# The last layer's main operations in one fixed order on three engines, with shorter forms at the ends of its rows

## The chip, the core and the metric

The kernel runs on one core of a Trainium2 chip. The metric is device time in microseconds (us) from the start of the program to its end. The engines are PE (TensorE: matrix products and transposes), DVE (VectorE: elementwise work and reductions), ACT (ScalarE: functions such as Ln and Exp, scaled copies), POOL (GpSimd) and SP (SyncE), which issues DMAs here. Each engine runs its own list of instructions in the order in which the program was emitted, and waits on semaphores for what other engines produce.

## What is computed

Four graph layers follow each other on x of 4096 rows and 64 features, with one 4096 x 4096 matrix adj in all of them. Each ends in `x = layernorm(x + layer(x))`. The change lies in the fourth layer and in the layernorm ahead of it. The fourth is a graph layer on the Poincare ball (c = 1):

```python
def _logmap(x, y, c):
    sub = _mobius_add(-x, y, c)
    sub_norm = jnp.maximum(jnp.linalg.norm(sub, axis=-1, keepdims=True), MIN_NORM)
    ...
    arg = jnp.clip(sqrt_c * sub_norm, 0.0, TANH_CLIP)
    return 2.0 / (sqrt_c * lam_x) * jnp.arctanh(arg) * sub / sub_norm
...
deg = jnp.maximum(adj.sum(axis=1, keepdims=True), 1e-08)
w = adj / deg
log_ij = _logmap(x[:, None, :], x[None, :, :], c)
agg = jnp.einsum('ij,ijc->ic', w, log_ij)
transformed = agg @ weight + bias
return _expmap(jnp.zeros_like(transformed), transformed, c)
```

So every pair (i, j) of the 4096 nodes needs a factor, a function of the distance of the two points; adj is multiplied by the factors, and the products with x are summed over j. The exponential map at the origin is tanh(|v|) v / |v|.

## The kernel before

**Layers 1 to 3** fill the first 957 us and are not touched, but for the layernorm behind layer 3. That is done for two groups of 512 rows at a time by ends() (L1397): summed (L1410) takes mean and variance by bn_stats and bn_aggr, roots (L1432) takes Ln and Exp on ACT, rest (L1436) refines the root by one step on DVE and applies it. Two of its four calls run as steps of a list called seam in the gather stage of layer 3, the other two as steps of the last layer's loop.

**The last layer's tiles.** The 4096 rows form eight groups of 512. The pairs form a triangle of 8 x 8 tiles of 512 x 512: row i of the triangle holds a diagonal tile (i, i) and the tiles (i, j) to its right, so there are rows of 8, 7, ... 1 tiles, 36 in all. The factor is symmetric, so a tile's factors serve twice: as they are, with adj's tile "own" (at_d), and transposed, with adj's opposite tile "mirrored" (at_m).

**Units.** A tile is worked in two units of 256 x 512, held as [128, 2, 512] (1024 elements in each of 128 partitions; the second unit of a diagonal tile has 512). The loop at L1846 takes one unit n an iteration, 72 in all, and works on several at once:

- product(n) (L1615): PE gives v, a bilinear form of the two points, in one of two PSUM places.
- square(n) (L1632): ACT writes w = v squared.
- opposite(n) (L1639): PE adds a term to v for the diagonal sign.
- less_one(n) (L1655): DVE lowers w by one and floors it.
- L1858, L1859: ACT takes Ln of w, then rt = Exp(0.5 Ln w), the root.
- L1883: DVE adds v and rt (in rt), after which v's place is free for product(n + 2).
- L1885: ACT turns w into Exp(-0.5 Ln w). L1894: ACT takes Ln of rt; in the program's text this is done for unit n - 1 at the end of iteration n.
- L1868: DVE forms the factors f = min(rt, T_MAX) w, for unit n - 2. L1871: DVE multiplies at_d by f.
- turn(t, h) (L1664): PE transposes f, eight blocks of 128 x 128 in an iteration (L1680, or L1673 on the diagonal), and DVE multiplies at_m by the result in PSUM (L1682, L1675).
- gather (L1685): PE sums own and mirrored products into one PSUM bank (L1696, L1704, L1708). ACT copies the mirrored half to tb (L1715) once a tile, and the row's own half at the end of the row (L1719).

The PSUM places: two for v (two banks each), three of one bank for transposes and all small products (tag "post"), one for the sums.

**Row ends.** When a row is complete, finals(g) (L1772) puts six steps on seam, and each iteration runs one: first (products with the weight), second (adds the bias), third (squares and norms by Ln and Exp), fourth (tanh as 1 - 2 / (1 + Exp 2|v|)) and fifth, which calls layernorm (L273) with by_ln and by_scale and issues the output's DMA on SP. The last three groups end after the loop (L1907).

**What sets the order.** A scheduler of the framework places the instructions of each engine; it keeps the data dependencies, and may move anything else. in_order() (L213) keeps an instruction in the program's order. behind(engine, ins) (L1387) adds a dependency without a semaphore on the instruction that was last passed to behind for that engine, so that all of them keep the order of the program's text. Before, only the start of the layer goes through behind: product for n < 2, opposite and less_one for n < 1, and the first instructions of ends().

Of the kernel before, what the change touches and what calls it, by code (L numbers as in the profile page):

```python
# [9 lines left out]
F32 = mybir.dt.float32  # L10
# [27 lines left out]

TANH_ONE = 20.0
# [23 lines left out]
def gnn4_kernel(  # L63
# [74 lines left out]
    nc.vector.memset(one_col, 1.0)  # L138

# [133 lines left out]
    def layernorm(dst, y, by_ln=False, by_scale=False):  # L273

        st = sm.tile([P, GB, 6], F32, name="ln_st")
        mv = sm.tile([P, GB, 2], F32, name="ln_mv")
        for b in range(GB):
            nc.vector.bn_stats(st[:, b, :], y[:, b, :])
            nc.vector.bn_aggr(mv[:, b, :], st[:, b, :])
        ve = sm.tile([P, GB], F32, name="ln_ve")  # L280
        s = sm.tile([P, GB], F32, name="ln_s")
        r = sm.tile([P, GB], F32, name="ln_r")
        nc.vector.tensor_scalar_add(ve, mv[:, :, 1], LN_EPS)
        if by_ln:
            nc.scalar.activation(s, ve, AF.Ln)
            nc.scalar.activation(s, s, AF.Exp, scale=0.5)
        else:
            nc.scalar.activation(s, ve, AF.Sqrt)

        nc.vector.reciprocal(r, s)  # L290
        nc.vector.tensor_tensor(r, ve, r, ALU.mult)
        nc.vector.tensor_tensor(s, s, r, ALU.add)
        nc.vector.reciprocal(r, s)
        nc.vector.tensor_scalar_mul(r, r, 2.0)
        if by_scale:
            nc.vector.scalar_tensor_tensor(s, mv[:, :, 0], -1.0, r, ALU.mult, ALU.mult)
            for b in range(GB):
                nc.scalar.activation(dst[:, b, :], y[:, b, :], AF.Identity, bias=s[:, b : b + 1], scale=r[:, b : b + 1])
            return
        nc.vector.tensor_tensor(dst, y, over_rows(mv[:, :, 0]), ALU.subtract)  # L300
        nc.vector.tensor_tensor(dst, dst, over_rows(r), ALU.mult)

# [1094 lines left out]
    def ends(two):  # L1397
# [12 lines left out]
        def summed(ps_p):  # L1410
# [19 lines left out]
            nc.vector.tensor_scalar_add(ve, mv[:, :, 1], LN_EPS)  # L1430

        def roots(ps_p):  # L1432
            nc.scalar.activation(s, ve, AF.Ln)
            nc.scalar.activation(s, s, AF.Exp, scale=0.5)

        def rest(ps_p):  # L1436

            nc.vector.reciprocal(r, s)
            nc.vector.tensor_tensor(r, ve, r, ALU.mult)
            nc.vector.tensor_tensor(s, s, r, ALU.add)  # L1440
            nc.vector.reciprocal(r, s)
            nc.vector.tensor_scalar_mul(r, r, 2.0)
# [127 lines left out]
    with tc.tile_pool(name="ps_v3", bufs=1, space=PSUM) as ps_v, tc.tile_pool(  # L1570
# [44 lines left out]
        def product(n):  # L1615
# [6 lines left out]
            for k in range(HB):  # L1622
                jb = j * CB + (n % 2) * HB + k
                half = slice(jb % 2 * F, jb % 2 * F + F)
                ins = nc.tensor.matmul(  # L1625
                    vs[n][:, k, cs], lhsT=tr_c[half, jb // 2, :], rhs=rights[i][0][half, cs], start=True, stop=True
                )
                in_order(ins)
                if n < 2:
                    behind("PE", ins)  # L1630

        def square(n):  # L1632
# [4 lines left out]
            nc.scalar.activation(ws[n][:, :, cs], vs[n][:, :, cs], AF.Square)  # L1637

        def opposite(n):  # L1639
# [4 lines left out]
            for k in range(HB):  # L1644
# [7 lines left out]
                if n < 1:  # L1652
                    behind("PE", ins)

        def less_one(n):  # L1655
            if n < NU:
# [4 lines left out]
                if n < 1:  # L1661
                    behind("DVE", ins)

        def turn(n):  # L1664
# [4 lines left out]
            if i == j:  # L1669
                tp = ps_p.tile([P, GW], F32, name="post", tag="post")  # L1670
                for k in range(HB):
                    for b in range(HB):
                        nc.tensor.transpose(tp[:, cols(HB * k + b)], fs[t][:, b, cols(HB + k)], ident)  # L1673
# [3 lines left out]
            for b in (HB * h, HB * h + 1):  # L1677
                tp = ps_p.tile([P, GW], F32, name="post", tag="post")
                for k in range(CB):
                    nc.tensor.transpose(tp[:, cols(k)], fs[t][:, k, cols(b)], ident)  # L1680
# [4 lines left out]
        def gather(t, h, tm):  # L1685
# [8 lines left out]
            for k in (HB * h, HB * h + 1):  # L1694
                if t is not None:
                    in_order(nc.tensor.matmul(  # L1696
# [3 lines left out]
                if tm is not None:  # L1700
                    above, below = tiles[tm]
                    if k == 0 and above != seq[0]:

                        in_order(nc.tensor.matmul(  # L1704
# [3 lines left out]
                    in_order(nc.tensor.matmul(  # L1708
# [63 lines left out]
        def finals(g):  # L1772
# [33 lines left out]
            def third(ps_p):  # L1806
# [7 lines left out]
                nc.scalar.activation(vn[:, :, 1], n, AF.Exp, scale=-0.5)  # L1814

            def fourth(ps_p):
                th = sm.tile([P, GB], F32, name="th")
                nc.vector.tensor_scalar_min(th, vn[:, :, 0], TANH_ONE)
                nc.scalar.activation(th, th, AF.Exp, scale=2.0)
                nc.vector.tensor_scalar_add(th, th, 1.0)  # L1820
                nc.vector.reciprocal(th, th)
                nc.vector.tensor_scalar(th, th, -2.0, 1.0, ALU.mult, ALU.add)
                nc.vector.tensor_tensor(th, th, vn[:, :, 1], ALU.mult)
# [3 lines left out]
            def fifth(ps_p):  # L1827
                o_sb = sm.tile([P, GB, F], F32, name="o_sb")
                layernorm(o_sb, v, by_ln=True, by_scale=True)
# [16 lines left out]
        while n < NU + 2 or turns or gathers:  # L1846
            if n % 2:
                load_own((n + 1) // 2)
                load_mirrored((n - 1) // 2)
            after = gather(*gathers.pop(n)) if n in gathers else []  # L1850
            turned = [w for what in turns.pop(n, []) for w in turn(what)]
            if n < NU:
# [5 lines left out]
                nc.scalar.activation(w, w, AF.Ln)  # L1858
                nc.scalar.activation(rt, w, AF.Exp, scale=0.5)  # L1859
                square(n + 1)  # L1860
                opposite(n + 1)
            if n >= 2 and n - 2 < NU:
# [5 lines left out]
                nc.vector.scalar_tensor_tensor(  # L1868
                    f, rts.pop(m)[:, :, cm], T_MAX, ws.pop(m)[:, :, cm], ALU.min, ALU.mult
                )  # L1870
                nc.vector.tensor_tensor(at, at, f, ALU.mult)  # L1871
# [8 lines left out]
            for work in turned:  # L1880
                work()
            if n < NU:
                nc.vector.scalar_tensor_tensor(rt, vs[n][:, :, cs], (1.0 + V_FLOOR) * SCALE, rt, ALU.max, ALU.add)  # L1883
                product(n + 2)
                nc.scalar.activation(w, w, AF.Exp, scale=-0.5)  # L1885
# [4 lines left out]
            for work in late:  # L1890
                work()
            if 0 < n <= NU:
                rt = rts[n - 1][:, :, columns(n - 1)]
                nc.scalar.activation(rt, rt, AF.Ln, scale=1.0 / SCALE)  # L1894
# [62 lines left out]
```

## Time and profile before

| | |
|---|---|
| median of 3 runs | 1388.71 us (1387.77 to 1390.9) |
| profiled execution | 1388.15 us, its span 1386.4 us |
| busy over the span | PE 93%, DVE 75%, ACT 58%, POOL 8% |
| granted TensorE clock, mean | 0.985 |
| last layer | from about 957 us to the end |
| its elementwise operations on 1024 elements | DVE 1.22 us each (f, at, rt), less_one 0.68; ACT 1.05 each |
| a mirrored product on 512 elements | DVE 0.68 us |

A line of the profile names the engine, the line of the kernel, the operation, and what it writes and reads (`out<-in`, partitions x elements). In a timeline, the first number is the start and the second the duration, in us from the start of the span; brackets hold the idle time of the engine just ahead of it and the instruction that ended it. A wait line reads: who waited, for whom, total us, how often, the longest. A row of the table by stretches gives start and end, length, and then for each engine its busy time and number of instructions, the clock, the share and the rate of the DMAs.

### The profile page before, as it was taken

How to read it: one execution, taken by the hardware profiler on the slowest of the kernel's cores; microseconds unless marked ns; L12 is line 12 of the kernel's file. 1: busy time of each engine (PE TensorE's matmuls, PEld its weight loads, DVE VectorE, ACT ScalarE, POOL GpSimd, SP SyncE). 2: the span in 40 equal slices, each digit the busy share in tenths (PEclk: the TensorE clock that was granted, in tenths of full speed). 3: DMA queues.
4: the chain of work that ended last, by engine and by line, in shares of the span. 5: the costliest groups of instructions: out<-in, count | busy, mean ns of one | idle time of the engine just before them, and what ended most of it. 6: DMA issues, size and time to landing. Idle time of an engine off the chain costs nothing.

```text
span 1386.4 us, 19115 instructions
## 1 busy us (share of the span) xinstructions
PE 1294.1 (93%) x6812; PEld 607.8 (44%) x6812; DVE 1045.7 (75%) x2004; ACT 806.1 (58%) x1346; POOL 114.2 (8%) x198
## 2 busy tenths in 40 slices
PE   9989999999999999999999999998888898988983
PEld 6655555565544334444444323333333333333431
DVE  7789999899434257787886223446999999999997
ACT  5544444344000115654424775656889999999994
POOL 3101111101123000010101000001000000000000
PEclk9999999999999999999999999998999999999998
DMA  9999999999799999999885855544245454445520
GB/s 345 372 408 410 405 410 410 410 407 391 282 388 367 390 417 375 421 367 350 324 319 183 240 173 179 159 147 167 99 161 197 172 212 152 186 156 190 191 83 12
DMA packets 108191, 382.16 MB, mean 276 GB/s; under 512 B 20276, under 2 KB 20280, under 8 KB 76472
## 3 DMA queue, kind: packets, MB, share of 16 engines
q1 hardware_dynamic: 90472, 297.03, 58.4%
q0 software_dynamic: 12736, 76.29, 13.3%
q10 hardware_dynamic: 4880, 7.54, 1.5%
q8 instruction: 56, 0.92, 0.3%
q14 instruction: 47, 0.39, 0.1%
HBM read 294.05 MB, written 85.20 MB: 274 GB/s over the span
## 4 chain that ended last, share of the span: by engine, by line
PE 58%; ACT 18%; DVE 13%; DMA 9%; issue 2%; SPq 1%; ACTq 0%; DVEq 0%
DMA raw<-in_adj_dram 8%; PE pass L574 7%; PE w_ps L574 5%; PE tp L738 5%; PE cnt_ps L1508 4%; PE a_last L1211 4%; PE a_ps L1211 4%; PE pass L567 4%; PE acc_ps L1468 4%; ACT rt L1859 3%; ACT w L1858 3%; ACT w L1637 3%; PE wide_last L1202 2%; PE p_ps L1202 2%; ACT w L1885 2%; ACT rt L1894 2%
## 5 line engine op out<-in xcount | busy, mean ns | idle before, releaser
L745 ACT COPY at<-tp 128x512 f32<-128x512 f32 x248 | 127.8, 599 | 123.0 <-issue 96.7
L1513 ACT ACTIVATE wt<-cnt_ps 128x512 uint16<-128x512 f32 x212 | 117.4, 595 | 64.1 <-PE cnt_ps L1508 61.8
L773 DVE TENSOR_REDUCE dpart<-raw 128x4 f32<-128x2048 f32 x64 | 145.4, 2273 | 7.1 <-DMA raw<-in_adj_dram 7.0
L1696 PE MATMUL sums_ps<-at_d,some 128*64 128x512 f32 x288 | 144.2, 622 | 4.5 <-ACT tb L1715 2.7
L775 DVE TENSOR_REDUCE lows<-raw 128x1 f32<-128x2048 f32 x64 | 145.4, 2272 | 0.0
L738 PE MATMUL tp<-ident,raw 128*128 128x128 f32 x1024 | 129.3, 279 | 11.2 <-DMA raw<-in_adj_dram 10.7
L738 PEld LDWEIGHTS tp<-ident,raw 128*128 128x128 f32 x1024 | 113.3, 142 | 48.5 <-issue 37.2
L1708 PE MATMUL sums_ps<-at_m,some 128*64 128x512 f32 x224 | 108.5, 605 | 0.0
L1625 PE MATMUL v_ps<-some,tr_a 64*128 64x512 f32 (+1 forms) x288 | 81.7, 644 | 21.2 <-DVE rt L1883 19.6
L574 PE MATMUL pass<-at,cheb_n 128*128 128x512 f32 x224 | 97.5, 593 | 0.5 <-DVE cheb_n L807 0.5
L574 PE MATMUL w_ps<-at,cheb_n 128*128 128x512 f32 x200 | 90.1, 593 | 0.0
L1883 DVE SCALAR_TENSOR_TENSOR rt<-v_ps,rt 128x1024 f32<-128x1024 f32 x72 | 83.2, 1155 | 5.0 <-ACT rt L1859 4.7
L1508 PE MATMUL cnt_ps<-m,follow 128*64 128x512 fp8e4 x480 | 82.0, 391 | 4.0 <-ACT wt L1513 1.4
L1868 DVE SCALAR_TENSOR_TENSOR f<-rt,w 128x1024 f32<-128x1024 f32 x72 | 83.3, 1157 | 0.9 <-ACT rt L1894 0.9
L1871 DVE TENSOR_TENSOR at_d<-at_d,f 128x1024 f32<-128x1024 f32 x72 | 83.2, 1155 | 0.1
L1682 DVE TENSOR_TENSOR at_m<-post,at_m 128x512 f32<-128x512 f32 x112 | 75.5, 680 | 3.5 <-PE post L1680 3.4
L1894 ACT ACTIVATE rt<-rt 128x1024 f32<-128x1024 f32 x72 | 72.2, 1004 | 8.8 <-DVE rt L1883 8.5
L1515 DVE TENSOR_SCALAR wt<-cnt_ps 128x512 uint16<-128x512 f32 x44 | 30.4, 691 | 61.8 <-PE cnt_ps L1508 61.8
L1680 PE MATMUL post<-ident,f 128*128 128x128 f32 x448 | 68.7, 284 | 6.2 <-DVE f L1868 2.9
L1696 PEld LDWEIGHTS sums_ps<-at_d,some 128*64 128x64 f32 x288 | 34.0, 139 | 89.1 <-issue 66.5
L1885 ACT ACTIVATE w<-w 128x1024 f32<-128x1024 f32 x72 | 72.4, 1006 | 0.7
L1859 ACT ACTIVATE rt<-w 128x1024 f32<-128x1024 f32 x72 | 72.3, 1004 | 0.6
(432 smaller groups left out, 2314.5 us busy)
## 6 DMA issues: line engine op xcount, KB each, us to landing
at<-adj_t SPq DMA_DIRECT2D x119, 1024.0 KB, 7.9
raw<-in_adj_dram SPq DMA_DIRECT2D x64, 1024.0 KB, 13.8
adj_t<-at POOLq DMA_DIRECT2D x62, 1024.0 KB, 8.0
at_d<-adj_t SPq DMA_DIRECT2D x36, 1024.0 KB, 4.8
at_m<-adj_t SPq DMA_DIRECT2D x28, 1024.0 KB, 6.9
m<-mask_t SPq DMA_DIRECT2D x120, 128.0 KB, 2.8
m<-mask_t SPq DMA_DIRECT2D x60, 256.0 KB, 3.4
mask_t<-mask ACTq DMA_DIRECT2D x28, 256.0 KB, 7.2
```

The lines of the kernel that those rows point to most:

```text
L574: in_order(nc.tensor.matmul(ps, lhsT=cheb_n[:, jb, k : k + 2, :], rhs=rhs, start=first, stop=last))
L738: in_order(nc.tensor.transpose(tp[:, cols(b)], raw[:, b, cols(k)], ident))
L745: nc.scalar.copy(at[:, k, :], tp)
L773: in_order(nc.vector.tensor_reduce(dpart[:, g, c, :], raw, AX.X, ALU.add))
L775: in_order(nc.vector.tensor_reduce(lows[:, n : n + 1], raw.rearrange("p b j -> p (b j)"), AX.X, ALU.min))
L1211: in_order(nc.tensor.matmul(ps[q * F : (q + 1) * F, :], lhsT=nat_a[:, c * CB + k, 0:F], rhs=of[q if signed else 0][:, k, :], start=(c == 0 ...
L1508: in_order(nc.tensor.matmul(cnt[a][r * HP : (r + 1) * HP, :], lhsT=follow, rhs=chunks[c][odd][2 * a + r][:, k, :], start=(h == 2 * NB - 1) ...
L1513: in_order(nc.scalar.activation(wt[odd][a], cnt[a], AF.Relu, scale=-128.0))
L1696: in_order(nc.tensor.matmul(bank[0:F, :], lhsT=nat_c[:, j * CB + k, :], rhs=own[t][:, k, :], start=(i == j and k == 0), stop=(j == seq[-1] ...
L1708: in_order(nc.tensor.matmul(bank[F:P, :], lhsT=nat_c[:, above * GB + k, :], rhs=mirrored[tm][:, k, :], start=(k == 0 and above == seq[0]), ...
L1859: nc.scalar.activation(rt, w, AF.Exp, scale=0.5)
L1885: nc.scalar.activation(w, w, AF.Exp, scale=-0.5)
```

## The change

1. behind() is now applied in every unit to all main operations: product, opposite, the transposes of turn() and the sums of gather() on PE; square, L1858, L1859, L1885 and L1894 on ACT; less_one, L1868, L1871, L1883 and the mirrored products on DVE. So they are emitted in the order of the program's text. Everything else (row ends, right()) is still placed by the scheduler.
2. In an iteration the transposes (turn) now come ahead of the sums (gather), and the mirrored products come after less_one instead of ahead of L1883.
3. The row ends and ends() take the inverse root as Exp(-0.5 Ln(var + eps)), the epsilon as the bias of the Ln, and refine it by one_more, three operations on DVE in place of six with the epsilon's. fourth() uses Exp(-2|v|) and loses its minimum and one more operation. Two constants are filled on POOL at the start.

```diff
-    def layernorm(dst, y, by_ln=False, by_scale=False):
+    def layernorm(dst, y):
...
+    def inverse_root(r, s, var):
+        nc.scalar.activation(s, var, AF.Ln, bias=small_var)
+        nc.scalar.activation(r, s, AF.Exp, scale=-0.5)
+
+    def one_more(r, s, var):
+        nc.vector.scalar_tensor_tensor(s, var, LN_EPS, r, ALU.add, ALU.mult)
+        nc.vector.scalar_tensor_tensor(s, s, -0.5, r, ALU.mult, ALU.mult)
+        nc.vector.scalar_tensor_tensor(r, s, 1.5, r, ALU.add, ALU.mult)
...
@@ ends(): roots and rest
-            nc.scalar.activation(s, ve, AF.Ln)
-            nc.scalar.activation(s, s, AF.Exp, scale=0.5)
+            inverse_root(r, s, mv[:, :, 1])
...
-            nc.vector.reciprocal(r, s)
-            nc.vector.tensor_tensor(r, ve, r, ALU.mult)
-            nc.vector.tensor_tensor(s, s, r, ALU.add)
-            nc.vector.reciprocal(r, s)
-            nc.vector.tensor_scalar_mul(r, r, 2.0)
+            one_more(r, s, mv[:, :, 1])
...
@@ product(); opposite() and less_one() likewise
-                if n < 2:
-                    behind("PE", ins)
+                behind("PE", ins)
...
@@ turn() and gather(): transposes and sums
-                    nc.tensor.transpose(tp[:, cols(k)], fs[t][:, k, cols(b)], ident)
+                    behind("PE", nc.tensor.transpose(tp[:, cols(k)], fs[t][:, k, cols(b)], ident))
...
-                    in_order(nc.tensor.matmul(
+                    behind("PE", nc.tensor.matmul(
...
@@ fourth()
-                nc.vector.tensor_scalar_min(th, vn[:, :, 0], TANH_ONE)
-                nc.scalar.activation(th, th, AF.Exp, scale=2.0)
+                nc.scalar.activation(th, vn[:, :, 0], AF.Exp, scale=-2.0)
                 nc.vector.tensor_scalar_add(th, th, 1.0)
                 nc.vector.reciprocal(th, th)
-                nc.vector.tensor_scalar(th, th, -2.0, 1.0, ALU.mult, ALU.add)
-                nc.vector.tensor_tensor(th, th, vn[:, :, 1], ALU.mult)
+                nc.vector.scalar_tensor_tensor(th, th, -0.5, vn[:, :, 1], ALU.add, ALU.mult)
...
@@ the loop
+            turned = [w for what in turns.pop(n, []) for w in turn(what)]
             after = gather(*gathers.pop(n)) if n in gathers else []
-            turned = [w for what in turns.pop(n, []) for w in turn(what)]
...
-                nc.scalar.activation(w, w, AF.Ln)
-                nc.scalar.activation(rt, w, AF.Exp, scale=0.5)
+                behind("ACT", nc.scalar.activation(w, w, AF.Ln))
+                behind("ACT", nc.scalar.activation(rt, w, AF.Exp, scale=0.5))
...
-                nc.vector.tensor_tensor(at, at, f, ALU.mult)
+                behind("DVE", nc.vector.tensor_tensor(at, at, f, ALU.mult))
...
-            for work in turned:
-                work()
...
             less_one(n + 1)
-            for work in late:
-                work()
+            for work in turned + late:
+                behind("DVE", work())
```

## Prediction

> **What bounds the kernel now.** I read the busy-by-slice rows of the page first: DVE and ACT are at nine tenths in the last third, where the last layer runs. Then the busy table of that stage, from the first less_one on DVE (957 us) to the end of its main operations (1362 us), and the drain behind it:
>
> ```profile
> core 0: us, PE busy (x) PEld busy (x) DVE busy (x) ACT busy (x) POOL busy (x), PEclk, DMA share, GB/s
> 957.00:1362.00 405.00, 357.23 (x1699) 151.77 (x1696) 388.11 (x652) 381.14 (x540) 13.42 (x19) 0.97 0.45 168
> 1362.00:1386.40 24.40, 3.99 (x24) 2.35 (x24) 16.16 (x85) 9.95 (x47) 0.00 (x0) 0.72 0.07 16
> ```
>
> DVE is idle 405.0 - 388.1 = 16.9 us of the stage, ACT 23.9. Two engines share the bound, so a better order can win 17 us at most. Where DVE's idle time lies, by the waits of DVE in the stage:
>
> ```profile
> DVE rt L1883 <- ACT rt L1859: 4.7, 7, 2.5
> DVE at_m L1682 <- PE post L1680: 3.4, 4, 1.2
> DVE w L1658 <- ACT w L1637: 3.0, 4, 1.1
> DVE nat_a L1420 <- PE post L1414: 1.2, 1, 1.2
> ```
>
> The columns are total, times, longest. Most of it is ACT being late; 3.4 us is the transposes (L1680) being late.
>
> **Short forms.** Small operations on [128, 4] last 0.16 us, but the next independent one starts much sooner, as the timeline of DVE shows (start, duration):
>
> ```profile
> 1100.02 0.16 DVE L294 TENSOR_SCALAR ln_r<-ln_r 128x4 f32<-128x4 f32 x1
> 1100.09 0.69 DVE L1682 TENSOR_TENSOR at_m<-post,at_m 128x512 f32<-128x512 f32 x1
> ```
>
> So one costs 0.07 us between large ones (a reciprocal 0.11). A row end loses the added epsilon, two reciprocals and three small products (0.50), gains the three steps of one_more (0.21), and in fourth() three become one (-0.14): -0.43. Five row ends lie in the stage: -2.15. Each of the two ends() in it loses 0.52 and gains 0.21: -0.6 for both. Sum -2.8; near row ends DVE partly waits for ACT anyhow, so I credit **-2**. ACT keeps its number of operations. The other two ends() lie in the gather stage before, where the chain of waits runs through PE (L1468, L1480): nothing. There an Ln now waits directly for bn_aggr and stands one Relu earlier on ACT; were the statistics late, the Relus queued behind it would hold PE, by 0.2 us a time. The two memsets are on POOL, 8% busy: nothing. "VectorE: DVE Perf Modes" of the Trainium skill (section "The DRAIN you can't avoid") has the next operation start only when the pipe is empty; by that the removed ones would be worth over twice as much, some -6 us, as an estimate from the 0.16 us above. The two rows above show the overlap, and the sum goes by them.
>
> **The fixed order, DVE.** In the emitted order of the changed kernel, each unit on DVE is f, at (L1871's product), rt, less_one, then the two mirrored products (L1682's). Before, the scheduler nearly always put something between f and the product that reads it. That matters:
>
> ```profile
> 1107.70 1.22 DVE L1868 SCALAR_TENSOR_TENSOR f<-rt,w 128x1024 f32<-128x1024 f32 x1
> 1108.83 0.68 DVE L1682 TENSOR_TENSOR at_m<-post,at_m 128x512 f32<-128x512 f32 x1
> 1109.43 1.22 DVE L1871 TENSOR_TENSOR at_d<-at_d,f 128x1024 f32<-128x1024 f32 x1
> ...
> 1351.59 1.23 DVE L1868 SCALAR_TENSOR_TENSOR f<-rt,w 128x1024 f32<-128x1024 f32 x1 [0.39 <-ACT rt L1894]
> 1352.85 1.23 DVE L1871 TENSOR_TENSOR at_d<-at_d,f 128x1024 f32<-128x1024 f32 x1
> ```
>
> An independent successor starts 1.13 us after f, the dependent one 1.26: it waits for the write. This bubble of 0.13 us stands in 4 of 72 units before and in 34 after (28 full, 6 half): 25 x 0.13 + 5 x 0.12 = **+3.9** of DVE time. At row ends a small operation fills the gap.
>
> **The fixed order, ACT.** Each unit is Ln w, Exp rt (reads w), Square, Exp w, Ln rt. Same effect:
>
> ```profile
> 1103.23 1.04 ACT L1858 ACTIVATE w<-w 128x1024 f32<-128x1024 f32 x1
> 1104.18 1.00 ACT L1637 ACTIVATE w<-v_ps 128x1024 f32<-128x1024 f32 x1
> ...
> 988.57 1.06 ACT L1858 ACTIVATE w<-w 128x1024 f32<-128x1024 f32 x1
> 989.66 1.06 ACT L1859 ACTIVATE rt<-w 128x1024 f32<-128x1024 f32 x1
> ```
>
> 0.95 apart when independent, 1.09 when not. Such pairs go from 18 to 63 (43 more full: +6.0, 2 more half: +0.3). Exp rt directly before Exp w, 1.08 apart, goes from 11 to 0: -1.4. Net **+4.9** of ACT time.
>
> **What the order does to the waits.** A unit in the middle of a row now takes DVE 1.26 + 1.13 + 1.13 + 0.60 + 2 x 0.60 = 5.32 us, ACT 1.09 + 0.95 + 0.91 + 0.95 + 0.95 = 4.85 plus a tb copy (0.6) in every second, 5.15 on average; PE (transposes 1.0, sums 1.9 to 2.3, opposite 0.4, product 1.1) at most 4.8. So DVE sets the pace there, and ACT can be at most about 1.3 us ahead (Exp rt done before DVE asks). The transposes now stand ahead of the sums on PE and their products at the unit's end on DVE, 3 us apart: the 3.4 us wait goes; late next is ACT. SP's loads keep their order. At a row end ACT gets 5.1 us more (v 1.0, squares 1.0, small Ln and Exp 0.7, o_sb 1.4, right 1.0, each from its spacing in the timeline) while DVE has no mirrored products for two units: over these units ACT needs some 2.4 us more than DVE, less the lead of 1.3: a stall of 1.1 us, and 0.2 at o_sb; more in short rows, where ACT can't get ahead again.
>
> The same as a ledger by rows. A tile off the diagonal costs DVE 2 x (3 x 1.13 + 0.60) + 4 x 0.60 = 10.39. A diagonal one costs 3.99 for the full unit, 2.13 for the half one and 0.60 for its own transposed product, and the row end 4.0 in the short form (seven of 256 elements at 0.33, the statistics 0.9, small ones 0.8): 10.7. So a row of k tiles takes DVE 10.39 (k - 1) + 10.7, then bubbles and stalls. Beside it stands the distance now, from the half-size rt (L1883) starts at 1056.29, 1132.14, 1198.72, 1253.56 and 1298.82 us in DVE's timeline:
> - 7 tiles: 73.0 + 0.9 + 1.3 = 75.2 (75.9 now); 6 tiles: 62.7 + 0.8 + 1.4 = 64.9 (66.6); 5 tiles: 52.3 + 0.6 + 1.5 = 54.4 (54.8); 4 tiles: 41.9 + 0.4 + 2.0 = 44.3 (45.3). Together **-3.8**, with bubbles and short forms inside.
> - First row: 12 bubbles (+1.6), the two ends() (-0.6), and a start in which rt(0) and less_one(1) now stand in line, with 3.5 us idle instead of 3.1 (0.69, 1.21, 0.67 and 0.56 now): **+1.4**.
> - Last three rows: two waits for transposes (1.13 and 1.22, at 1336.6 and 1343.1) go, bubbles come: **-1.5**.
>
> **The drain.** After 1362 us three row ends run on dependent steps 0.2 us apart:
>
> ```profile
> 1379.33 0.17 DVE L283 TENSOR_SCALAR ln_ve<-ln_mv 128x4 f32<-128x4 f32 x1
> ...
> 1380.51 0.18 DVE L290 RECIPROCAL ln_r<-ln_s 128x4 f32<-128x4 f32 x1 [1.02 <-ACT ln_s L286]
> 1380.72 0.16 DVE L291 TENSOR_TENSOR ln_r<-ln_ve,ln_r 128x4 f32<-128x4 f32 x1
> ```
>
> On the last one five steps become three (-0.4), the minimum ahead of the Exp goes (-0.25), one product goes (-0.2), the epsilon goes (-0.2), and ACT's four o_sb no longer split the squares of the group behind (-0.4): -1.45, called **-1.3** for what queues behind other groups' steps.
>
> **Sum.** -3.8 + 1.4 - 1.5 - 1.3 = -5.2. The profiled execution took 1388.15 us (span 1386.4 and 1.75 around it), 0.56 under the median of the runs, 1388.71. So about **1383.0** us, 0.4% under the median. The ledger's weak term is the stalls: the four rows now lose 1.7 to 2.9 us each over DVE's own work, and I give them 1.3 to 2.0. If they lost as much as now on top of the bubbles, the end would be some 4 us later; if nothing, some 6 us earlier.
>
> **Rivals.**
> - *Trade without gain*, 1388: the rows keep their stalls (+4, and 1 more in the first and last rows), so the +3.9 and +4.9 of bubbles eat what the removed waits give. For it: both engines are over 94% busy, and the present order avoids these bubbles. Against: the wait for transposes and the drain are clear gains.
> - *Order nearly perfect*, 1377: row-end stalls fall to nothing as well (-6). Against: ACT's excess at row ends stays.
> - *Slower*, 1395: Ln rt is now last on ACT, behind the tb copy or o_sb, and f heads DVE's queue and waits for it, with at, rt and less_one behind, and Ln w behind those. When ACT has no lead, Ln rt ends 0.91 + 0.95 + 0.6 + 1.05 = 3.5 us after Exp rt, DVE wants it after 2.93: 0.6 us a copy. It decides once the lead of 1.3 us is used up beyond the row ends; in 20 of the 28 copy units that is +12 on the forecast. Against: 5.32 over 5.15 restores the lead. "PSUM — Partial Sum Buffer" of the Trainium skill (section "Engine vs sequencer instructions") has the queues of ScalarE and VectorE strictly first in, first out, so that a waiting head holds all behind it; it gives no price, and no row of this trace tells it from a scheduler's choice.
> - *The order isn't as said*: the emitted order shows that it is; without it only the forms are left, -2 and the drain's -1.3: 1385.
>
> **Chances.** 0.2% is 2.8 us, about what a measurement can tell from no change; faster is under 1385.9, slower over 1391.5. Forecast 0.50 (1380 to 1387; 0.43 of it faster), trade 0.19 (0.17 same, 0.02 faster), perfect 0.16, slower 0.15 (0.13 slower). Faster 0.61, same 0.26, slower 0.13. The range is 1375.5 to 1391.5: it takes in both ends of the ledger, and leaves out a little of the perfect case and most of the slow one.
>
> **What would show it.** DVE busy in the last layer near 389 us and ACT near 386; f to at 1.26 us apart in 34 of the 72 units; no at_m waiting for transposes; DVE's waits nearly all for Exp rt, at row ends; the drain some 1.3 us shorter. Wrong if f waits for Ln rt in mid-row, or if PE makes anyone wait.

## The result, and the profile after

The changed kernel is slower: 1395.78 us median (1393.44 to 1399.22, 10 runs) against 1389.55 (1387.10 to 1393.62, 10 runs) for the kernel before; ratio 1.0041, 95% interval [1.0024, 1.0057]. The forecast was 1383.0. The profiled execution took 1396.61 us (span 1394.9; before 1388.15 and 1386.4).

The line numbers move: product L1623, Square L1634, opposite L1645, less_one L1655, transposes L1676 (L1669 on the diagonal), their products L1678 (L1671), Ln w L1864, Exp rt L1865, f L1874, at L1877, rt L1887, Exp w L1889, Ln rt L1898; in ends() the products of summed L1418, their addition L1424.

The busy table of the changed kernel, same columns as before (the drain now ends at 1395):

```profile
957.00:1362.00 405.00, 346.53 (x1661) 153.01 (x1661) 379.47 (x607) 381.36 (x526) 12.80 (x21) 0.96 0.44 168
1362.00:1395.00 33.00, 12.50 (x65) 6.43 (x64) 23.60 (x86) 14.89 (x63) 0.00 (x0) 0.82 0.06 12
```

In the same 405 us DVE works 379.5 us, 8.6 less than before. It has not become faster: with the drain its busy time is nearly the same (403.1 against 404.3 us). It waits more. DVE's waits from 955 to 1372 us (total, times, longest):

```profile
DVE nat_a L1424 <- PE post L1418: 8.1, 2, 5.4
DVE rt L1887 <- ACT rt L1865: 5.4, 7, 2.2
DVE f L1874 <- ACT rt L1898: 5.1, 8, 1.3
DVE at_d L1671 <- PE post L1669: 4.0, 5, 1.9
DVE w L1655 <- ACT w L1634: 1.9, 3, 0.7
```

The wait of at_m for transposes is gone, as forecast. Three others have grown: for the products of summed (1.2 before), f for Ln rt (0.9 before), the diagonal's product for its transposes (0.7 before). The largest lies at the start of the layer. TensorE there, in the changed kernel:

```profile
961.57 0.40 PE L1645 MATMUL v_ps<-wq_signed,some 64*128 64x256 bf16 x2 [3.08 <-ACT w L1634]
962.35 2.08 PE L1623 MATMUL v_ps<-some,tr_a 64*128 64x512 f32 x4 [0.38 <-DVE rt L1887]
964.36 3.67 PE L1418 MATMUL post<-wd,sums 128*128 128x64 f32 x16
```

The products of summed (L1418) need nothing that is late, but they were emitted behind opposite(1), which waits for Square, and behind product(2), which waits for rt(0). So they start at 964.36. VectorE of the same kernel:

```profile
962.21 0.42 DVE L1655 TENSOR_SCALAR w<-w 128x512 f32<-128x512 f32 x1
968.07 0.69 DVE L1424 TENSOR_TENSOR nat_a<-post,tr_a 128x512 f32<-128x512 f32 x1 [5.44 <-PE post L1418]
968.67 0.68 DVE L1887 SCALAR_TENSOR_TENSOR rt<-v_ps,rt 128x512 f32<-128x512 f32 x1
```

The addition heads VectorE's queue for 5.44 us, and rt(1), whose Exp rt ended at 963.95, stands behind it. In the kernel before the same products ran at 957.56 to 959.9, ahead of product(2):

```profile
957.56 0.44 PE L1414 MATMUL post<-wd,sums 128*128 128x64 f32 x2
957.93 0.28 PE L1647 MATMUL v_ps<-wq_signed,some 64*128 64x256 bf16 x2
958.14 1.77 PE L1414 MATMUL post<-wd,sums 128*128 128x64 f32 x14
...
962.89 1.91 PE L1625 MATMUL v_ps<-some,tr_a 64*128 64x512 f32 x4 [1.81 <-DVE rt L1883]
```

By the marks of the prediction's ledger (starts of the half-size rt, and the layer's first rt), in us, each from one profile:

| | first rt to second | first row | 7 | 6 | 5 | 4 | 3 | 2 tiles | to the end | last layer in all |
|---|---|---|---|---|---|---|---|---|---|---|
| before | 2.7 | 92.0 | 75.9 | 66.6 | 54.8 | 45.3 | 31.6 | 23.6 | 32.4 | 424.9 |
| after | 7.6 | 94.2 | 76.4 | 65.9 | 55.4 | 46.0 | 34.5 | 22.3 | 31.4 | 433.8 |

The "last layer" (span less the first rt's start) leaves out what lies ahead of it, which varies between executions (last section). Of the 9.0 us lost, 7.0 are lost by the end of the first row (101.77 against 94.75 from the first rt).

### The profile page after: what moved, and what is told of

Read it like the earlier page. It is cut to its first block, busy times and chain, and to the rows that moved or that the text cites. A ratio compares the mean times of both kernels' runs of the same rounds, so it can differ in the third digit from the quotient of the medians.

```text
span 1394.9 us, 19099 instructions
## 1 busy us (share of the span) xinstructions
PE 1290.9 (93%) x6812; PEld 612.3 (44%) x6812; DVE 1043.4 (75%) x1952; ACT 810.4 (58%) x1346; POOL 112.7 (8%) x200
## 4 chain that ended last, share of the span: by engine, by line
PE 59%; ACT 16%; DVE 14%; DMA 6%; issue 4%; ACTq 0%; DVEq 0%; SPq 0%
PE pass L578 7%; PE w_ps L578 6%; DMA raw<-in_adj_dram 6%; PE tp L742 5%; PE cnt_ps L1506 4%; PE a_ps L1215 4%; PE pass L571 4%; PE acc_ps L1466 4%; PE a_last L1215 4%; DVE rt L1887 3%; PE p_ps L1206 2%; ACT rt L1865 2%; ACT w L1864 2%; ACT wt L1511 2%; PE wide_last L1206 2%
## 5 line engine op out<-in xcount | busy, mean ns | idle before, releaser
L1623 PE MATMUL v_ps<-some,tr_a 64*128 64x512 f32 (+1 forms) x288 | 78.6, 622 | 30.6 <-DVE rt L1887 27.5
L1887 DVE SCALAR_TENSOR_TENSOR rt<-v_ps,rt 128x1024 f32<-128x1024 f32 x72 | 83.4, 1159 | 5.5 <-ACT rt L1865 5.4
L1874 DVE SCALAR_TENSOR_TENSOR f<-rt,w 128x1024 f32<-128x1024 f32 x72 | 83.4, 1159 | 5.4 <-ACT rt L1898 5.1
L1877 DVE TENSOR_TENSOR at_d<-at_d,f 128x1024 f32<-128x1024 f32 x72 | 83.7, 1163 | 1.2
L1864 ACT ACTIVATE w<-w 128x1024 f32<-128x1024 f32 x72 | 72.3, 1004 | 13.4 <-DVE w L1655 13.0
L1865 ACT ACTIVATE rt<-w 128x1024 f32<-128x1024 f32 x72 | 72.7, 1010 | 2.0
L1678 DVE TENSOR_TENSOR at_m<-post,at_m 128x512 f32<-128x512 f32 x112 | 72.6, 684 | 0.0
L1898 ACT ACTIVATE rt<-rt 128x1024 f32<-128x1024 f32 x72 | 72.1, 1001 | 0.2
L1889 ACT ACTIVATE w<-w 128x1024 f32<-128x1024 f32 x72 | 72.1, 1001 | 0.0
L1676 PE MATMUL post<-ident,f 128*128 128x128 f32 x448 | 67.6, 293 | 4.3 <-ACT some L1388 2.8
```

Of the source, the lines that this page charges most:

```text
L1865: behind("ACT", nc.scalar.activation(rt, w, AF.Exp, scale=0.5))
L1887: behind("DVE", nc.vector.scalar_tensor_tensor(rt, vs[n][:, :, cs], (1.0 + V_FLOOR) * SCALE, rt, ALU.max, ALU.add))
```

## The experiments

Theory A: the loss is the place of summed in the chains. B: the fixed order loses in every row, by bubbles and by waits at row ends. C: the short forms cost. A2 and D, for what is left after A: heads of VectorE's queue, or ScalarE's order. Ratios are to the kernel before, run beside it; they need not equal the quotient of the medians (e13: 0.9986, with medians of 1388.91 and 1388.10). The kernel before gave medians of 1388.10 to 1390.06 beside the five groups of runs, so medians of different groups (e1 to e4, e5 to e8, e9 to e12, e13 to e16, e17 and e18) can differ by 2 us for that alone. The last layer comes from one profile a run.

| | median, us | ratio [95%] | last layer, us |
|---|---|---|---|
| changed kernel | 1395.78 | 1.0041 [1.0024, 1.0057] | 433.8 |
| e1 forms only | 1386.45 | 0.9981 [0.9968, 0.9995] | 422.4 |
| e2 sum free | 1392.24 | 1.0022 [1.0012, 1.0032] | 426.8 |
| e3 less_one between f and at | 1413.34 | 1.0179 [1.0165, 1.0193] | 450.0 |
| e4 Ln rt early | 1395.52 | 1.0041 [1.0028, 1.0054] | 430.8 |
| e5 sum and late product free | 1391.15 | 1.0006 [0.9992, 1.0020] | 423.6 |
| e6 = e5 + e4 | 1384.88 | 0.9965 [0.9953, 0.9976] | 421.2 |
| e7 = e6, mirrored between f and at | 1382.81 | 0.9961 [0.9947, 0.9976] | 419.8 |
| e8 = e2, ScalarE's chain off | 1399.05 | 1.0070 [1.0057, 1.0083] | 436.0 |
| e9 forms, and the start's chain | 1391.28 | 1.0011 [0.9996, 1.0025] | 430.9 |
| e10 forms, transposes first | 1393.47 | 1.0033 [1.0018, 1.0047] | 430.0 |
| e11 = e7, Exp w between Ln w and Exp rt | 1390.80 | 1.0006 [0.9989, 1.0023] | 425.8 |
| e12 = e5 again | 1389.29 | 0.9986 [0.9966, 1.0006] | 425.5 |
| e13 products of summed free | 1388.91 | 0.9986 [0.9972, 1.0001] | 426.9 |
| e14 addition of summed free | 1394.22 | 1.0033 [1.0018, 1.0048] | 430.5 |
| e15 = e7, summed chained | 1392.11 | 1.0015 [0.9998, 1.0032] | 429.3 |
| e16 = e7 again | 1383.33 | 0.9944 [0.9924, 0.9965] | 421.7 |
| e17 = e7, transposes behind the sums | 1496.70 | 1.0762 [1.0737, 1.0787] | 534.9 |
| e18 = e7, long forms | 1387.71 | 0.9998 [0.9986, 1.0010] | 423.6 |

### e1: the forms alone

The changed kernel with every order as before:

```diff
-                behind("PE", ins)
+                if n < 2:
+                    behind("PE", ins)
...
-                behind("ACT", nc.scalar.activation(w, w, AF.Ln))
+                nc.scalar.activation(w, w, AF.Ln)
```

> The kernel before with the short row-end forms alone (inverse_root, one_more, the shorter fourth and fifth); every order as before. Theory A (the loss is the start of the last layer: the products of summed and their addition now stand in the same chains as all main operations, behind product(2) on TensorE and at the head of VectorE's queue): the forms are worth 0 to 4 us, so 1386 to 1389.5. Theory B (the fixed order loses in every row, by bubbles and by VectorE's waits for Ln rt and Exp rt at row ends): the same, 1386 to 1389.5. Theory C (the short forms themselves cost): 1394 or more.

1386.45, 2.7 us under the kernel before (1389.15 beside it). Theory C falls: the forms gain, and the order costs 9.3 us (1395.78 - 1386.45; by the ratios some 8).

### e2, e13, e14: the sum out of the chains

```diff
 # summed: e2 both, e13 the first, e14 the second
-                    if begun:
+                    if False:
                         behind("PE", ins)
...
-            if begun:
+            if False:
                 behind("DVE", ins)
```

> The changed kernel, with the products of summed and their addition taken out of the two chains, everything else in the fixed order. Theory A: VectorE's two waits for these products (5.4 and 2.6 us in the profile, 1.2 before) go, 6 to 8 us less than the changed kernel: 1388 to 1390, level with the kernel before. Theory B: the time comes back as waits further on, 0 to 2 us less: 1394 to 1396. Theory C: no change, 1396.

> The changed kernel with only the products of summed (TensorE) taken out of their chain; their addition stays in VectorE's chain, behind rt(0) and less_one(1). If TensorE's place makes the start's loss (the products wait behind product(2), which waits for rt(0)): the second rt comes 3 to 4 us after the first, as in e2, the time 1391 to 1393. If VectorE's place makes it: 7.6 us between the two, 1395 to 1396.

> The changed kernel with only the addition of summed (VectorE) taken out of its chain; the products stay in TensorE's, behind product(2). The scheduler now puts rt(1) ahead of the addition. If the addition at the head of VectorE's queue makes the loss: second rt 3 to 4 us after the first and 1391 to 1393. If the late products make it, since the addition and what follows it still wait for them: the wait only moves behind rt(1), first row as long as in the changed kernel, 1394 to 1396.

With both free the last layer is 7.1 us shorter than in the changed kernel. The median is only 3.5 less, 1392.24, above the 1388 to 1390 of theory A. From the second row on each distance is the changed kernel's to 0.1 us (76.4, 65.9, 55.4, 46.0, 34.5, 22.3): B's "it comes back later" falls. With TensorE's products alone free, the layer is as short (426.9; median 1388.91, level with the kernel before, and less than the 1391 to 1393 expected). The sixteen products then run from 957.1 to 959.6 us, and the addition doesn't wait. VectorE of e13:

```profile
961.44 0.42 DVE L1655 TENSOR_SCALAR w<-w 128x512 f32<-128x512 f32 x1
961.77 0.69 DVE L1424 TENSOR_TENSOR nat_a<-post,tr_a 128x512 f32<-128x512 f32 x1
```

With VectorE's addition alone free, rt(1) moves ahead, but the wait only moves too. VectorE of e14:

```profile
963.27 0.69 DVE L1887 SCALAR_TENSOR_TENSOR rt<-v_ps,rt 128x512 f32<-128x512 f32 x1 [1.36 <-ACT rt L1865]
967.35 0.69 DVE L1424 TENSOR_TENSOR nat_a<-post,tr_a 128x512 f32<-128x512 f32 x1 [3.39 <-PE post L1418]
```

Its first row takes 96.8 us, 4.8 more than before; from the first rt that is 5.0 of the changed kernel's 7.0. So it is TensorE's place that costs: VectorE's adds some 2 us while the products are late, and nothing once they are free (e13).

### e9, e15: that place put into other kernels

```diff
 # e9, in e1: product, opposite, less_one and rt
-                if n < 2:
+                if n < 3:
                     behind("PE", ins)
...
-                if n < 1:
+                if n < 2:
                     behind("PE", ins)
...
+                if n < 2: behind("DVE", ins)
```

> e1_forms_only (before's orders, short forms) with the chains of before carried on over the first two units alone: product up to n=2, opposite and less_one up to n=1, and rt of units 0 and 1. So the products of summed stand behind product(2) on TensorE and their addition behind rt(0) on VectorE, as in the changed kernel; every later order is the scheduler's. Theory A (this place alone makes the start's part of the loss): the first rt to the second 5 us longer than in e1, 7.6 against 2.7 us, and the time 4 to 6 us above e1, 1390 to 1392.5. If the start's loss needs the fixed order behind it: 1386 to 1388, like e1.

> e7 with the products of summed and their addition put back into the chains, as the change has them. If the start's loss adds to the later rows' whatever these do: 7 us more last layer than e7 (419.8), and 1387 to 1390. If e7's gains in the later rows came from the free sum: 1393 or more.

e9: 7.6 us from first rt to second, as in the changed kernel, and 1391.28, 4.8 above e1 (last layer 8.5). e15 stands 8.8 us above e16, run beside it, and above the 1387 to 1390 that I expected; the start and the first row make 8.8 us of that, and the later rows are alike to 1.1 us. The place costs about as much with a free order behind it (e9, 8.5 us of last layer), the changed order (e2, 7.1) and a mended one (e15: 7.6 against e16, 9.4 against e7).

### e4, e5, e12, e6: what is left, at the row ends

```diff
 # e4: Ln rt of unit n-1 ahead of Exp w of unit n
                 product(n + 2)
+                if n: r1 = rts[n - 1][:, :, columns(n - 1)]; behind("ACT", nc.scalar.activation(r1, r1, AF.Ln, scale=1.0 / SCALE))
                 behind("ACT", nc.scalar.activation(w, w, AF.Exp, scale=-0.5))
...
 # e5, on e2: the diagonal's transposes and its late product out of the chains
-            for work in turned + late:
-                behind("DVE", work())
+            for work in turned: behind("DVE", work())
+            for work in late: work()
```

> The changed kernel with Ln rt of the unit before ahead of Exp w in ScalarE's order, not behind it, so that the f that heads VectorE's queue has one ScalarE operation (1.0 us) more of slack at the row ends; all else as changed. Theory A: f's waits for Ln rt were 5.1 us in 8 places; a part of them goes, the start stays: 1392 to 1395. Theory B (row-end waits are the loss): 1390 or less. The wait may also move to rt or to at only: then 1395 to 1397.

> The changed kernel with the sum free as in e2_sum_free, and also the diagonal tile's turned factors (the transposes of turn for a diagonal tile and the product L1671) out of the chains. In e2 VectorE still waits 5.9 us in 5 places for these transposes, which stand on TensorE behind product(n+2), with all of VectorE's main operations behind the product; before the change this wait was 0.7. Theory A2 (what is left of the loss are these heads of VectorE's queue): 3 to 5 us less than e2, 1387 to 1389.5. Theory D (ScalarE's order at the row ends sets the pace, VectorE's waits are what it leaves): 1391 to 1393.

> The kernel of e5 a second time. Its last layer (first rt to the end) was 3.2 us shorter than that of e2, its median only 1.1 less, as its part ahead of the layer took 967 us in the profile where the others took 960 to 964. If that part varies from one execution to the next: last layer 423.6 again, and a median of 1387 to 1390. If it belongs to this kernel: 1391 again.

> e5 and Ln rt of the unit before ahead of Exp w. In e4 this took 3.0 us off the last layer's length in the profile, all of it in the later rows, though the median moved by only 0.3. Theory A2: 1 to 3 us less than e5. Theory D: the row ends gain as they did in e4, 1 to 3 us less than e5. No gain if the waits for Ln rt and those for the diagonal's transposes were the same stretches of time.

How Ln rt comes late, in the changed kernel: ScalarE, then VectorE, at one row end.

```profile
1313.98 0.58 ACT L1711 COPY tb<-sums_ps 64x512 f32<-64x512 f32 x1 [0.95 <-PE sums_ps L1704]
1314.57 0.58 ACT L1715 COPY tb<-sums_ps 64x512 f32<-64x512 f32 x1
1315.05 0.63 ACT L1898 ACTIVATE rt<-rt 128x512 f32<-128x512 f32 x1
```

```profile
1315.71 0.69 DVE L1874 SCALAR_TENSOR_TENSOR f<-rt,w 128x512 f32<-128x512 f32 x1 [1.26 <-ACT rt L1898]
```

The copies, which wait for PE, stand ahead of Ln rt, which f waits for. Taken alone, e4 makes the layer 3.0 us shorter and the median 0.3: outside the 1392 to 1395 that I expected, inside the 1395 to 1397 of a wait that only moves. In its profile no wait of f for Ln rt is left, and rt's for Exp rt is 7.0 us instead of 5.4. e5's median was 1.1 under e2, below the expected 3 to 5; read again (e12) it was 3.0 under. The two readings of one kernel differ by 1.9 us in both median and last layer, and in opposite directions, so a single step of this size is at the edge of what is told apart here. Both steps together (e6) are not: 1384.88, 4.4 under the lower reading of e5 and e12 and 7.4 under e2. VectorE's waits for Ln rt and for the diagonal's transposes, in e2 and then in e6:

```profile
DVE at_d L1671 <- PE post L1669: 5.9, 5, 2.2
DVE f L1874 <- ACT rt L1898: 5.0, 9, 1.0
```

```profile
DVE at_d L1671 <- PE post L1669: 0.7, 1, 0.7
DVE f L1874 <- ACT rt L1889: 0.5, 2, 0.2
```

A part of it comes back: rt's wait for Exp rt goes from 3.3 to 5.8 us. So B was right on the row ends, in the size of 5 us, and wrong on the larger part of the loss. What of this is Ln rt's and what the diagonal's stays open.

### e3, e7, e16, e11: the bubbles

```diff
 # e3: Square ahead of Exp rt, less_one ahead of at (e7: a mirrored product there)
                 behind("ACT", nc.scalar.activation(w, w, AF.Ln))
-                behind("ACT", nc.scalar.activation(rt, w, AF.Exp, scale=0.5))
                 square(n + 1)
+                behind("ACT", nc.scalar.activation(rt, w, AF.Exp, scale=0.5))
...
+                less_one(n + 1)                                    # e3
+                if turned: behind("DVE", turned.pop(0)())          # e7
                 behind("DVE", nc.vector.tensor_tensor(at, at, f, ALU.mult))
...
-            less_one(n + 1)                                        # e3
+            less_one(n + 1) if n < 2 or n - 2 >= NU else None      # e3
...
 # e11, on e7
                 behind("ACT", nc.scalar.activation(w, w, AF.Ln))
+                if n: w1 = ws[n - 1][:, :, columns(n - 1)]; behind("ACT", nc.scalar.activation(w1, w1, AF.Exp, scale=-0.5))
                 behind("ACT", nc.scalar.activation(rt, w, AF.Exp, scale=0.5))
...
-                behind("ACT", nc.scalar.activation(w, w, AF.Exp, scale=-0.5))
```

> The changed kernel with another fixed order inside each unit: Square of the next unit between Ln w and Exp rt on ScalarE, less_one of the next unit between f and at on VectorE, so that no operation directly follows the one whose result it reads; the start as in the changed kernel. Theory A: the waits of the start stay, only the bubbles go (0.13 us in 34 units of VectorE, some 4 us where VectorE sets the pace): 1391 to 1394. Theory B: the bubbles and the late Exp rt are the loss: 1389 or less. If ScalarE sets the pace, or Exp rt one operation later holds rt up by as much: 1395 to 1398.

> e6 with the first mirrored product put between f and at on VectorE, instead of behind less_one: mid-row no VectorE operation reads the one just before it, and the recurrence from rt over product and Square to less_one is left alone (e3 put less_one there, and TensorE and ScalarE had to follow it in turn). If the bubble of 0.13 us in some 34 units sets the pace: 3 to 4.5 us less than e6. If VectorE only fills its bubble and then waits for Exp rt (ScalarE sets the pace): 0 to 1 us less. If rt, now 0.6 us later behind f, holds up product(n+2): 0 to 3 us more.

> The kernel of e7 a second time, beside the others of this call: e12 showed that the same kernel's last layer and median can differ by 2 us between two runs, as much as e7 stood below e6 (1382.8 and 1384.9). If e7 is the fastest kernel: 1381.5 to 1384 again, below e1 (1386.5). If not: 1384 to 1387.

> e7 with Exp w of the unit before put between Ln w and Exp rt on ScalarE, so that Exp rt no longer directly follows the operation whose result it reads (1.09 against 0.95 us). If ScalarE's bubbles set the pace, as the prediction's ledger had them (0.14 us in some 60 places): 3 to 8 us less than e7, 1375 to 1380. If VectorE sets it and Exp rt, one operation later, makes rt wait: 0 to 6 us more, 1383 to 1389.

e3 puts an independent instruction into each of these gaps and is 17.6 us slower than the changed kernel, which none of the expectations reached. Its waits:

```profile
PE v_ps L1623 <- DVE rt L1887: 68.9, 57, 3.4
ACT w L1634 <- PE v_ps L1623: 24.5, 29, 2.1
DVE w L1655 <- ACT w L1634: 19.1, 27, 1.7
```

In the changed kernel the first of them is 27.5 us in 36 places. Each waits for the one above, and rt stands behind less_one: rt(n), product(n+2), Square(n+2), less_one(n+2), at, rt(n+1) form a ring that must turn once a unit: 1.13 + 1.13 + 1.0 + 0.6 + 1.13 = 5.0 us of work, and the hand-overs between three engines besides. The row of 7 tiles took 80.1 us instead of 76.4. Exp rt, which e3 also puts one operation later, is hardly it: rt waits for it 6.7 us in 6 places (5.4 in 7 in the changed kernel). In the changed order less_one(n+2) stands behind rt(n+1), so that the ring has a unit more. e7 fills VectorE's bubble without touching the ring: only 3 pairs of f and at are left adjacent, of 36 in e6. It takes 2.1 us off e6, with e16's reading 1.5; in last layer the two lie 1.4 under and 0.4 over e6. That is no more than two readings of one kernel differ. The forecast price of those bubbles was 4. e11 fills ScalarE's bubble and loses 8 us (4 to 6 in last layer): rt waits for Exp rt 16.4 us in 22 places (5.0 in 10 in e7). There it matters who waits for Exp rt, not what stands between two instructions of ScalarE.

### e8, e10, e17, e18: which part of the change is worth what

e8 is e2 without any behind("ACT", ...); e18 is e7 with the long forms of before (a part shown); e10 is e1 and e17 is e7, each with two lines swapped:

```diff
 # e8
-                behind("ACT", nc.scalar.activation(rt, w, AF.Exp, scale=0.5))
+                nc.scalar.activation(rt, w, AF.Exp, scale=0.5)
...
 # e18
-            inverse_root(r, s, mv[:, :, 1])
+            nc.scalar.activation(s, ve, AF.Ln)
+            nc.scalar.activation(s, s, AF.Exp, scale=0.5)
...
 # e17 (e10 the reverse)
-            turned = [w for what in turns.pop(n, []) for w in turn(what)]
             after = gather(*gathers.pop(n)) if n in gathers else []
+            turned = [w for what in turns.pop(n, []) for w in turn(what)]
```

> e2 with ScalarE's chain taken out (its order is the scheduler's again), TensorE's and VectorE's fixed. Theory D (ScalarE's fixed order is what is left of the loss): 1386 to 1389. Theory A2 (it is VectorE's and TensorE's order): 1391 to 1394.

> e1_forms_only with one line moved: a unit's transposes of factors are issued ahead of its sums, as in the change, and nothing is chained. The prediction gave this part the end of VectorE's waits for the transposes (3.4 us before). If that holds outside the fixed order: 1 to 3 us less than e1, 1383.5 to 1385.5. If the sums now come late and hold product and opposite up: 0 to 3 us more than e1.

> e7 (now read twice: 1382.8 and 1383.3) with a unit's transposes of factors issued behind its sums again, as before the change; all chains as in e7. In e10 the transposes ahead, in an order that was otherwise the scheduler's, cost 7 us. If the transposes ahead of the sums are worth their place inside a fixed order, as the prediction had it: VectorE waits for them again, 3 us or more above e7, 1386 to 1390. If they cost there too: 1376 to 1381.

> e7 with the long row-end forms of before: the mended order alone, without the short forms. If the forms and the order add, with the 2.7 us that e1 measured for the forms: 1385 to 1387. If the short forms are worth more once the order is mended: 1387 to 1389. If less: 1383 to 1385.

e8: theory D is not borne out, and the time is above what either theory gave. Without ScalarE's chain the scheduler puts Ln rt so early that it waits for rt (16.9 us in 38 places), and rt then waits for Exp rt (22.0 in 23); 6.8 us more than e2. That the scheduler's order of ScalarE is worse doesn't make the fixed one good: another fixed order, with Ln rt early, gains (e6). e10: the transposes ahead, in the scheduler's order, cost 7.0 us, more than the 0 to 3 expected, and VectorE still waits 3.1 us for them (2.4 in e1); its waits of less_one for Square grow from 7.9 to 11.0 us. What delays Square there was not followed up. e17: behind the sums, in the mended fixed order, they cost 113 us, where I had expected 3 or more. Its waits:

```profile
DVE at_m L1678 <- PE post L1676: 115.8, 54, 4.5
ACT w L1864 <- DVE w L1655: 113.2, 52, 4.8
```

A mirrored product, fixed between f and at, now waits in 54 places for transposes that wait behind the sums, and ScalarE waits for less_one behind it. (In the changed kernel the mirrored products stand later; what the same swap would cost there was not tried.) e18: the mended order with the long forms takes 1387.71, ratio 0.9998: no different from before. The short forms on top of that order give 4.4 to 4.9 us (e16, e7; in last layer 1.9 to 3.8), on the old order 2.7 (e1; 2.4).

## Why the prediction was wrong

For the last layer the sum gave -5.2 us, and the profiles measure +9.0. Of the 14.2 us between them 5.6 lie in the first row, 5.1 in the rows of 7 to 4 tiles, 3.2 in the last rows and 0.3 in the drain. So two steps failed: the place of summed, which the prediction had wrong and which alone makes the kernel slower, and the stalls at the row ends, which were to shrink and didn't. With the first mended alone (e13) the kernel is level with the one before, not 0.4% under it.

**First row, +1.4: the step that made it slower.** I gave the start "3.5 us idle instead of 3.1", with rt(0) and less_one(1) in line ahead of the addition of summed. I had followed VectorE's emitted order only. On TensorE the products of summed had moved behind product(2), which waits for rt(0). Start and first row together measured +7.0. e13 takes all of it away at that one place; e9 and e15 put it in elsewhere. The section on the kernel before names the place: the first instructions of ends() went through behind() already, when nothing in the chain waited for rt.

**Rows of 7 to 4 tiles, -3.8.** Measured +1.3 (243.8 against 242.5). Mid-row units took 5.32 us, as worked out, to 5.6, and there were 34 adjacent pairs of f and at, 1.24 to 1.26 us apart where they are full:

```profile
1104.65 1.22 DVE L1874 SCALAR_TENSOR_TENSOR f<-rt,w 128x1024 f32<-128x1024 f32 x1
1105.91 1.23 DVE L1877 TENSOR_TENSOR at_d<-at_d,f 128x1024 f32<-128x1024 f32 x1
```

The stalls at row ends, which the prediction called the ledger's weak term, were mis-sized: I gave them 1.3 to 2.0 us a row; the distance less the ledger's work and bubbles (73.9, 63.5, 52.9, 42.3) leaves 2.5, 2.4, 2.5 and 3.7. In these rows rt's waits for Exp rt fell from 3.6 to 2.0 us and less_one's for Square from 2.6 to 0.7. In their place the diagonal's product waits 3.1 us for its transposes (nothing before), which the ledger had at nothing, and f 2.0 for Ln rt (0.3 before), which it had left to a rival. With the diagonal's product free and Ln rt early (e6) the four rows take 241.7.

**Last three rows, -1.5.** The rows of 3 and 2 tiles measured +1.7 (56.9 against 55.2; the row of one tile lies in the table's column "to the end"). The waits for transposes went, as forecast, but the row of 3 tiles took 2.9 more, with f waiting for Ln rt (2.6 us) and rt for Exp rt (1.1). Of those 2.9 us 1.3 may not be the change's: two profiles of one kernel (e5, e12) have 33.2 and 34.5 us in that row.

**Drain, -1.3.** Measured -1.0 from the last half-size rt. On the last group the five steps are three, as forecast:

```profile
1389.39 0.16 DVE L303 SCALAR_TENSOR_TENSOR ln_s<-ln_mv,ln_r 128x4 f32<-128x4 f32 x1 [1.31 <-ACT ln_r L299]
1389.59 0.16 DVE L304 SCALAR_TENSOR_TENSOR ln_s<-ln_s,ln_r 128x4 f32<-128x4 f32 x1
1389.79 0.16 DVE L305 SCALAR_TENSOR_TENSOR ln_r<-ln_s,ln_r 128x4 f32<-128x4 f32 x1
```

**Short forms, -2 and the drain's -1.3.** About right: e1 measured -2.7 with the old order, e18 against e7 and e16 -4.4 to -4.9 with the mended one. The estimate of some -6 from "VectorE: DVE Perf Modes" of the Trainium skill (section "The DRAIN you can't avoid") was not reached with either. The same section says that a next operation that isn't held starts earlier, which the prediction left out and which the 0.07 us of its two rows agree with.

**Bubbles, +3.9 and +4.9.** Their number was right, their price not: without most of VectorE's (e7, e16) the gain was at most 1.5 to 2.1 us, which can't be told from nothing, and taking ScalarE's away (e11) lost 8. A gap on an engine costs only as far as that engine sets the pace there, and what fills it may be late for somebody else.

**The transposes ahead of the sums.** Their 3.4 us wait went, as forecast, but only together with the fixed order: with the scheduler's order they cost 7.0 us (e10).

**The rivals.** The slower one named the kind, a waiting head of VectorE's queue, but put it on f and Ln rt in mid-row; f's waits were 5.1 us, all but 0.3 of it where a row end's steps run. It gave 1395, and the kernel took 1395.8 by another mechanism: that the number fits is luck. That the queue of VectorE is strictly first in, first out ("PSUM — Partial Sum Buffer" of the Trainium skill, section "Engine vs sequencer instructions") agrees with the traces: rt(1) waited behind the addition until 968.67 us in the changed kernel, and in e14 it ran at 963.27, as soon as it stood ahead of the addition in the order. "Wrong if PE makes anyone wait" was the right test.

What the change would give if mended: e7 and e16, 1382.8 and 1383.3, the forecast's own figure, by an order that the forecast didn't describe; but by e18 the order's part of that can't be told from nothing without the short forms.

## What to carry to other kernels

When a fixed order is spread over more instructions, list everything that already stands in the same chain and ask of each what now stands ahead of it, on the producer's engine as well as on the consumer's: one set of products without any late input, emitted behind one that waits, cost 7 us of a 425 us layer. Read an order across engines, as rings of who waits for whom (rt, product, Square, less_one), before filling gaps on one engine. And run the parts alone: here the short forms gained by themselves, the transposes ahead of the sums cost 7.0 us by themselves, and the fixed order, which lost 113 us without those transposes ahead (e17), was worth nothing without the short forms (e18).

## What the runs showed of the hardware

The granted clock of TensorE fell to half around a stretch without work, which lengthened the wait. The changed kernel from 959 us, then e13, whose products run without the idle stretch ahead of them (columns as in the busy table; the clock is the third number from the end):

```profile
959.00:963.00 4.00, 1.05 (x4) 0.61 (x5) 1.56 (x2) 3.77 (x5) 1.70 (x4) 0.61 1.00 412
963.00:967.00 4.00, 4.00 (x17) 2.65 (x13) 0.00 (x0) 3.41 (x5) 0.00 (x0) 0.50 1.01 426
```

```profile
959.00:963.00 4.00, 3.17 (x24) 2.14 (x23) 2.67 (x8) 3.97 (x7) 0.93 (x3) 1.00 1.00 418
963.00:967.00 4.00, 1.66 (x6) 0.50 (x6) 3.60 (x17) 3.97 (x8) 0.00 (x0) 0.81 1.01 428
```

At 0.50 the sixteen products took 3.67 us; the second set, from 992.8 us at 1.00, took 2.00. A product() of four matmuls took 2.08 us from 962.35 and 1.13 from 991.76. So of the 5.44 us of waiting some 2.6 are the clock's, as an estimate from these two pairs (3.67 - 2.00 and 2.08 - 1.13). In the kernel before the clock fell as well (0.51 from 963 to 967 us), but the products were done by then. The page "TensorE: Matmul & The Clock Gate" of the Trainium skill (section "Part 1: The HAM clock gate") has two states, full and half, with half after an idle window of about 3.4 us. The rows show the half, but not an idle time of 3.4 us ahead of it: in rows of half a microsecond the clock of the changed kernel falls at 959.9 us, 1.4 us after the last matmul, and that of e13 at 965.5, 0.7 us after work had resumed behind 2.1 us without any. What the window counts, and how long it is, no run here shows.

What lies ahead of the last layer is not constant: its first rt started between 959.6 and 967.4 us, and for one and the same kernel at 966.9 (e5) and 962.0 (e12). In those two profiles the transfers from 100 to 200 us ran at 389 and 409 GB/s. So a median can move less, or more, than the last layer; what sets those rates was not looked into.
